# Attention values computed in pairs of steps, with one more buffer of exponentials and fewer of cross queries, in a kernel whose order comes from a list planner

## The chip, the cores and the metric

The kernel runs on one NeuronCore of a Trainium2 chip. The metric is the device time of one execution in microseconds, given as the median of several runs. A profile comes from one further execution of the same program, whose own time stands beside its span.

## The reference

Two blocks follow each other. The inputs are x (16 batches, 256 tokens, 256 features) and a context (16 batches, 77 tokens, 256 features), all in float32.

The first block is a transformer layer with 16 heads of 16 features:

```
h = x + attention(rmsnorm(x), rmsnorm(x))        # self, 256 keys
h = h + attention(rmsnorm(h), context)           # cross, 77 keys
h = h + (silu(n @ w_gate) * (n @ w_up)) @ w_down # n = rmsnorm(h), 1024 wide
attention: softmax(q k^T / 4) v per head, then @ wo
```

The second block takes h as queries and the context as keys and values. It normalizes both, attends with one head, squeezes through a layer of 4 features (gelu), attends among the 256 tokens of a batch with the result, and adds the parts to the normalized queries.

## The kernel before

**Units and batches.** Two batches make a unit of 512 tokens. The residual h of a unit stays in one of four buffers (`BUFS["h"]`, L82) from its load (L94) to its store (L1068). Everything else is per batch, except the cross keys and the final block, which work on a unit.

**Attention.** Queries and keys of a batch lie transposed, as two chunks of 128 features with 8 heads each. Each head pair takes 32 partitions. The partitions that the other head of the pair occupies are masked to zero, and one of them carries the row maximum as an extra product term.
- `self_operands` (L612) projects queries, keys and values (psq, psk, psv).
- `self_maxima` (L465) computes scores once for their maxima: four steps sc of 8 matmuls on row groups, each reduced on VectorE (L482). `cross_maxima` (L491) does the same with two steps csc.
- `maxima_rows` (L449) transposes the maxima (tm, ctm) and puts them into the queries.
- `exponentials` (L517) computes the scores again, with keys on partitions (st, cst), and ScalarE takes the exponential into a tile pT (L544). Self attention has four such steps per batch: two chunks of heads by two halves of the keys. Cross attention has two, one for each chunk, since 77 keys fit into one half.
- `outputs` (L549) multiplies values with exponentials (po, cpo), one step for each step of exponentials: 8 matmuls on column groups of the array, accumulated over the key halves in one bank, then a 32x32 transpose on VectorE (L576).
- `projection` (L578) divides by the sums, transposes and multiplies with wo (wo, cwo). `cross_queries` (L681) normalizes h, transposes (tp_ca) and projects cross queries (pscq), which ScalarE copies three times: into cqT as they are (L690), and masked into cqx (L692).

**MLP and final block.** `mlp` (L696) transposes (tp_mlp), multiplies with gate and up (pg, pu), passes tanh on ScalarE and two products on VectorE, and multiplies with down (wd). `second_context` (L860) and `second` (L896) make the final block, a long chain of small steps (tp_nF, xsc, tpxp, xav, tp_g2T, tp_mgT, lsc, lst, lav, tp_lav, out).

**PSUM.** There are eight banks: a tile of four for scores on row groups (`sc_banks`, one buffer, so each such step waits for the reading of the previous one), one for values (`po_bank`), and a ring of three for all else (`mm_bank`).

**The order.** Each stage is a generator that yields steps (`Step`, L223). A step states its duration on PE, its shape ("f" for the full array, "r" for row groups, "c" for column groups), its bank, its work on other engines, and the resources that it needs, takes and frees. `Order.run` (L310) picks at each point the PE step with the best key: steps that could start within a set waiting time (`wait`, L320) come first, then the rank. Ranks are the batch's number plus an offset by stage (`RANKS`, L1097), with further offsets for the first two and the last three batches. The buffers in `BUFS` limit how many tiles of a kind may be in flight. The four compute engines' queues then stand in exactly this order[...]. Loads and stores stand on SyncE's queue.

Three resources matter for the change. The ring of exponential tiles pT has two buffers, shared by self and cross attention. The resource "pair" (limit 1) keeps the exponentials of one group of steps from being mixed with another's: `acq` at the first key half, `rel` at the last. And the cross queries' tiles cqT and cqx have two buffers each.

Of the kernel before, what the change touches and what calls it, by code (L numbers as in the profile page):

```python
# [15 lines left out]
P = 128  # L16
D = 256
NC = D // P
# [4 lines left out]
UB = 2  # L23
RG = 32
# [5 lines left out]
def kernel(  # L30
# [10 lines left out]
    nc = tc.nc  # L41
    B, S, _ = x.shape
# [18 lines left out]
    def mm_bank(name):  # L61
        return ps_mm.tile([P, 512], F32, tag="mm", name=name)

    def po_bank(name):
        return ps_po.tile([P, 2, S], F32, tag="po", name=name)

    def sc_banks(name):
        return ps_sc.tile([P, 4, 512], F32, tag="sc", name=name)
# [8 lines left out]
    def tokens(ap, u):  # L77
# [2 lines left out]

    BUFS = {
        "h": 4, "cx": 1, "cx2": 2, "hn": 3, "hnT_sa": 1, "hnT_ca": 1, "hnT_mlp": 1, "ctxT": 1,  # L82
        "qx": 3, "kx": 3, "vone": 3, "cqT": 2, "cqx": 2, "ckm": 1, "ckx": 1, "cvone": 2, "pT": 2,
        "po": 1,
        "os": 2, "oq": 1, "oT": 1, "sg": 2, "gT": 1,
    }
# [129 lines left out]
    T_S, T_ST, T_CS, T_CST, T_PV = 816, 816, 478, 774, 740  # L216
# [6 lines left out]
    class Step:  # L223
        def __init__(self, pe=0, shape="f", bank="mm", ops=(), needs=(), acq=(), rel=(),
                     gives=(), order=None, free=False, lag=0, part=0):
            self.pe, self.shape, self.bank, self.ops, self.needs = pe, shape, bank, ops, needs
            self.acq, self.rel, self.gives = acq, rel, gives
            self.order, self.free, self.lag = order, free, lag

            self.part = part  # L230
# [6 lines left out]
    class Order:  # L237
# [72 lines left out]
        def run(self):  # L310
            while self.streams:
                best = None
                aux = []
                for st in self.streams:
                    t = self.start(st)
                    if t is None:
                        continue
                    if st.step.pe:

                        wait = 20 if "f" in (self.shape, st.step.shape) else 100  # L320
                        late = t > self.clock["P"] + wait
                        key = (late, t if late else 0, st.rank)
                        if best is None or key < best[0]:
                            best = (key, st, t)
                    else:
                        e = st.step.ops[0][0]
                        aux.append((max(t + T_NEXT, self.clock[e]), st.rank, st, t))
                if aux:
                    b, _, st, t = min(aux, key=lambda a: a[:2])
                    if best is None or b + sum(o[1] for o in st.step.ops) <= best[2] + best[1].step.pe + 800:  # L330
                        self.put(st, t)
                        continue
                assert best, [(st.rank, vars(st.step)) for st in self.streams]
                self.put(best[1], best[2])
# [95 lines left out]
    class Attention:  # L430
# [3 lines left out]
        def __init__(self, b, name, nk, w):  # L434
            self.b, self.name, self.nk, self.w = b, name, nk, w
            self.steps = [
                (c, kc, min(P, nk - kc * P)) for c in range(NC) for kc in range(-(-nk // P))
            ]
            self.q = self.k = self.qx = self.kx = self.v = None
            self.pT = {}  # L440

        def key(self, what, *more):
            return (self.name + what, self.b, *more)
# [44 lines left out]
    def last_of_pair(a):  # L488
        return a.b % UB == UB - 1
# [27 lines left out]
    def exponentials(a):  # L517

        b = a.b
        for k, (c, kc, nk) in enumerate(a.steps):  # L520
            last = k == len(a.steps) - 1
            rel = [(a.name + "qx", a.b)]
            if not a.name:
                rel.append(("kx", b))
            elif last_of_pair(a):
                rel.append(("ckx", b // UB))
            yield Step(
                T_CST if a.name else T_ST, "r", "sc", ops=[("A", 1870)], free=True,
                needs=[a.key("mT")] + [(a.name + "pT", b - 1, len(a.steps) - 1)] * (b > 0), acq=[("pT", a.name, a.b, k)] + [("pair",)] * (kc == 0),
                rel=[("pair",)] * (kc == (a.nk - 1) // P) + rel * last, gives=[a.key("pT", k)],  # L530
            )
            st = sc_banks(f"{a.name}st{a.b}_{k}")
            groups = [slice(RG * j, RG * (j + 1)) for j in range(4)]
            for e in range(2):
                for j, rg in enumerate(groups):
                    nc.tensor.matmul(  # L536
                        st[:nk, j, e * S : (e + 1) * S],
                        lhsT=a.kx[rg, c, e, kc * P : kc * P + nk], rhs=a.qx[rg, c, e],
                        start=True, stop=True,
                    )  # L540
            a.pT[k] = pool.tile(
                [P, 4, 2, S], F32, tag="pT", name=f"{a.name}pT{a.b}_{k}", bufs=BUFS["pT"]
            )
            nc.scalar.activation(  # L544
                a.pT[k][:nk].rearrange("p j e q -> p j (e q)"), st[:nk], AF.Exp,
                scale=HD ** -0.5,
            )

    def outputs(a):  # L549

        n = a.name
        for k, (c, kc, nk) in enumerate(a.steps):
            first, end = kc == 0, (kc + 1) * P >= a.nk
            yield Step(
                T_PV, "c", None, ops=[("V", 690)] if end else [], free=True,
                order=("pT", n, a.b, k), needs=[a.key("pT", k), a.key("v")],
                acq=[("po",)] * first + [("os", n, a.b)] * (end and c == 0),
                rel=[("pT", n, a.b, k)] + [("po",)] * end
                + [("cvone" if n else "vone", a.b)] * (k == len(a.steps) - 1),
                gives=[a.key("os", c)] * end,  # L560
            )
            if first:
                po = po_bank(f"{n}po{a.b}_{c}")
            pT = a.pT.pop(k)
            for e in range(2):
                for j in range(4):
                    nc.tensor.matmul(  # L567
                        po[RG * j : RG * (j + 1), e, :],
                        lhsT=a.v[:nk, kc, 8 * c + 2 * j + e, :], rhs=pT[:nk, j, e, :],
                        start=(first and e == 0), stop=end, skip_group_check=True,  # L570
                    )
            if end:
                if c == 0:
                    a.os = a.tile("os", [P, 2, NC, S], shared=True)

                nc.vector.transpose(a.os[:, :, c], po)  # L576

    def projection(a):  # L578

# [505 lines left out]
    def second_loads():  # L1085
# [4 lines left out]
    order = Order({**BUFS, "pair": 1})  # L1090
# [6 lines left out]
    RANKS = {  # L1097
        "loads": (-3, 0, 0),
        "second_constants": (1, 50, 0),
        "outputs": (1.5, 0, 0),  # L1100
        "exponentials": (-1.5, 0, 0),
        "projection": (1.25, 0, 0),
        "cross_outputs": (3, 0, 0),
        "cross_exponentials": (-50, 0, 0),
        "cross_projection": (-50, 0, 0),
        "self_maxima": (-1, 0, -50),
        "cross_maxima": (-49, 0, 0),
        "cross_queries": (1.75, 0, -1),
        "self_operands": (-1.5, 0, 1.5),
        "cross_keys": (2, 0, 0),  # L1110
        "mlp": (4.25, 0.25, -1),
        "second_context": (4, 0, -50),
        "second": (1, 0, 0),
    }

    def add(stage, b, tie, gen):
# [9 lines left out]
    for b in range(B):  # L1126
        a, ca = Attention(b, "", S, wo), crosses[b]
        add("outputs", b, 0, outputs(a))
        add("exponentials", b, 1, exponentials(a))
        add("projection", b, 2, projection(a))  # L1130
        add("cross_outputs", b, 0, outputs(ca))
        add("cross_exponentials", b, 1, exponentials(ca))
        add("cross_projection", b, 2, projection(ca))
        add("self_maxima", b, 1, self_maxima(a))
        add("cross_maxima", b, 1, cross_maxima(ca))
        add("cross_queries", b, 3, cross_queries(ca))
        add("self_operands", b, 5, self_operands(a))
        if b % UB == 0:
            add("cross_keys", b, 5, cross_keys(crosses[b : b + UB]))
        add("mlp", b, 4, mlp(b))  # L1140
# [43 lines left out]
```

## Time and profile before

| | |
|---|---|
| median of 3 runs | 1015.22 us (1014.69 to 1019.04) |
| profiled execution | 1016.78 us |
| its span, first to last instruction | 1015.0 us |
| mean granted TensorE clock | 0.985 |
| DVE reductions of sc (L482) | 64 of 2287 ns |
| exponentials of st (L544) | 64 of 1875 ns |
| exponentials of cst (L544) | 32 of 1872 ns |
| DMA | 17.58 MB, 16 engines mostly idle after the start |

The profile names an instruction by its line, engine, operation and tiles (output<-inputs), without buffer numbers. A float32 matmul is two records on PE, and a transpose is one; so "x8" of a projection is four matmuls of the program. In the timeline a row gives its start and its length in us, then what it is. The length of a PE row is modelled at its end, and rows overlap; the distance between the starts of two rows is what PE really takes. The slices show a span in 40 parts. In the chain of waits each piece is what the next one waited for.

### The profile page before, as it was taken

How to read it: one execution, taken by the hardware profiler on the slowest of the kernel's cores; microseconds unless marked ns; L12 is line 12 of the kernel's file. 1: busy time of each engine (PE TensorE's matmuls, PEld its weight loads, DVE VectorE, ACT ScalarE, POOL GpSimd, SP SyncE). 2: the span in 40 equal slices, each digit the busy share in tenths (PEclk: the TensorE clock that was granted, in tenths of full speed). 3: DMA queues.
4: the chain of work that ended last, by engine and by line, in shares of the span. 5: the costliest groups of instructions: out<-in, count | busy, mean ns of one | idle time of the engine just before them, and what ended most of it. 6: DMA issues, size and time to landing. Idle time of an engine off the chain costs nothing.

```text
span 1015.0 us, 18822 instructions
## 1 busy us (share of the span) xinstructions
PE 971.6 (96%) x8115; PEld 702.6 (69%) x8115; DVE 587.8 (58%) x1003; ACT 509.1 (50%) x876; POOL 80.7 (8%) x117
## 2 busy tenths in 40 slices
PE   6888899999999999999999999999999999999995
PEld 5655566767666777777777777767676777777872
DVE  3765674647775576645757356647466465345542
ACT  4545645452744626455373637553664627434432
POOL 2100000000100001000010001000010001000110
PEclk9999999999999999999999999999999999999995
DMA  9100000000000100010000100010000000000000
GB/s 297 34 1 7 1 1 2 2 8 1 1 8 8 43 1 8 2 43 1 7 2 13 42 1 1 7 43 1 8 8 2 22 1 2 1 22 1 2 21 22
DMA packets 17348, 17.58 MB, mean 17 GB/s; under 512 B 2832, under 2 KB 16752, under 8 KB 17264
## 3 DMA queue, kind: packets, MB, share of 16 engines
q1 hardware_dynamic: 16144, 15.32, 4.9%
q8 instruction: 64, 1.05, 0.4%
q10 hardware_dynamic: 1088, 1.05, 0.3%
q14 instruction: 20, 0.16, 0.1%
q0 software_dynamic: 32, 0.00, 0.0%
HBM read 12.13 MB, written 4.19 MB: 16 GB/s over the span
## 4 chain that ended last, share of the span: by engine, by line
PE 83%; DVE 8%; ACT 5%; DMA 3%; issue 1%; POOL 0%; ACTq 0%; POOLq 0%; SPq 0%
PE wd L746 11%; PE pu L717 10%; PE pg L717 10%; PE st L536 6%; PE sc L477 6%; PE po L567 5%; PE cst L536 3%; PE cwo L605 3%; PE psq L403 3%; PE cpo L567 3%; PE wo L605 3%; DVE nmax L482 2%; PE psv L637 2%; PE psk L403 2%; ACT pT L544 2%; PE pscq L403 2%
## 5 line engine op out<-in xcount | busy, mean ns | idle before, releaser
L482 DVE TENSOR_REDUCE nmax<-sc 128x8 f32<-128x2048 f32 x64 | 146.4, 2287 | 36.6 <-PE sc L477 36.5
L544 ACT ACTIVATE pT<-st 128x2048 f32<-128x2048 f32 x64 | 120.0, 1875 | 73.9 <-PE st L536 73.7
L717 PE MATMUL pg<-hnT_mlp,wg 128*128 128x256 f32 x512 | 129.3, 387 | 0.0
L717 PE MATMUL pu<-hnT_mlp,wu 128*128 128x256 f32 x512 | 128.5, 386 | 0.0
L746 PE MATMUL wd<-wd,gT 128*128 128x256 f32 x512 | 126.0, 387 | 0.0
L746 PEld LDWEIGHTS wd<-wd,gT 128*128 128x128 f32 x512 | 92.5, 190 | 23.5 <-issue 12.1
L717 PEld LDWEIGHTS pu<-hnT_mlp,wu 128*128 128x128 f32 x512 | 93.5, 190 | 20.3 <-issue 8.7
L717 PEld LDWEIGHTS pg<-hnT_mlp,wg 128*128 128x128 f32 x512 | 92.7, 190 | 20.0 <-issue 8.6
L727 ACT ACTIVATE sg<-pg 128x512 f32<-128x512 f32 x64 | 38.1, 596 | 98.0 <-PE pg L717 97.6
L544 ACT ACTIVATE cpT<-cst 77x2048 f32<-77x2048 f32 x32 | 59.9, 1872 | 54.5 <-PE cst L536 54.5
L728 DVE SCALAR_TENSOR_TENSOR sg<-sg,pg 128x512 f32<-128x512 f32 x64 | 43.9, 686 | 70.4 <-ACT sg L727 69.9
L567 PE MATMUL po<-pT,vone 128*32 128x256 f32 x1024 | 67.3, 391 | 0.0
L510 DVE TENSOR_REDUCE nmax<-csc 128x16 f32<-128x1232 f32 x32 | 46.1, 1441 | 17.1 <-PE csc L503 16.6
L729 DVE SCALAR_TENSOR_TENSOR gT<-sg,pu 128x512 f32<-128x512 f32 x64 | 43.6, 681 | 18.0 <-PE pu L717 17.2
L567 PEld LDWEIGHTS po<-pT,vone 128*32 128x32 f32 x1024 | 28.5, 111 | 28.8 <-issue 15.3
L751 DVE TENSOR_TENSOR h<-h,wd 128x256 f32<-128x256 f32 x32 | 13.3, 417 | 50.7 <-PE wd L746 50.6
L197 POOL TENSOR_TENSOR rstd_n<-ve_n,neg_half 128x4 f32<-128x4 f32 (+2 forms) x26 | 22.4, 862 | 242.2 <-DVE ve_n L195 235.5
L403 PE MATMUL psq<-hnT_sa,wq 128*128 128x256 f32 x128 | 34.8, 410 | 0.6 <-ACT hnT_sa L363 0.6
L567 PE MATMUL cpo<-cpT,cvone 77*32 77x256 f32 x512 | 34.3, 385 | 0.3 <-DVE cos__7617 L576 0.3
L403 PE MATMUL psk<-hnT_sa,wk 128*128 128x256 f32 x128 | 32.6, 390 | 0.0
L403 PE MATMUL pscq<-hnT_ca,cwq 128*128 128x256 f32 x128 | 32.4, 390 | 0.0
L197 POOL TENSOR_TENSOR rstd_ca<-ve_ca,neg_half 128x2 f32<-128x2 f32 x16 | 11.1, 694 | 263.2 <-DVE ve_ca L195 263.2
(601 smaller groups left out, 1567.2 us busy)
## 6 DMA issues: line engine op xcount, KB each, us to landing
h<-in_x_dram SPq DMA_DIRECT2D x7, 512.0 KB
out_dram<-h SPq DMA_DIRECT2D x7, 512.0 KB
cx<-in_ctx_dram SPq DMA_DIRECT2D x16, 154.0 KB
wg<-in_L_xattn_w_gate_dram SPq DMA_DIRECT2D x1, 1024.0 KB
wu<-in_L_xattn_w_up_dram SPq DMA_DIRECT2D x1, 1024.0 KB
wd<-in_L_xattn_w_down_dram SPq DMA_DIRECT2D x1, 1024.0 KB
h<-in_x_dram SPq DMA_DIRECT2D x4, 128.0 KB
out_dram<-h SPq DMA_DIRECT2D x2, 256.0 KB
```

The lines of the kernel that those rows point to most:

```text
L403: nc.tensor.matmul(ps[:, m * n : (m + 1) * n], lhsT=w[:, c, m * P : (m + 1) * P], rhs=srcT[:, c, :], start=(c == 0), stop=(c == NC - 1),)
L477: nc.tensor.matmul(sc[:, j, (1 - e) * S : (2 - e) * S], lhsT=a.qx[rg, c, e, qt * P : (qt + 1) * P], rhs=a.kx[rg, c, e], start=True, stop=True,
L482: nc.vector.tensor_reduce(maxima_of(nm, qt)[:, :, c::NC], sc.rearrange("p j (y k) -> p j y k", y=2), AX.X, ALU.max, negate=True,)
L510: nc.vector.tensor_reduce(maxima_of(nm, qt), sc[:, :, : 2 * NC * SK].rearrange("p j (n k) -> p j n k", k=SK), AX.X, ALU.max, negate=True,)
L536: nc.tensor.matmul(st[:nk, j, e * S : (e + 1) * S], lhsT=a.kx[rg, c, e, kc * P : kc * P + nk], rhs=a.qx[rg, c, e], start=True, stop=True,)
L544: nc.scalar.activation(a.pT[k][:nk].rearrange("p j e q -> p j (e q)"), st[:nk], AF.Exp, scale=HD ** -0.5,)
L567: nc.tensor.matmul(po[RG * j : RG * (j + 1), e, :], lhsT=a.v[:nk, kc, 8 * c + 2 * j + e, :], rhs=pT[:nk, j, e, :], start=(first and e == 0 ...
L605: nc.tensor.matmul(ps[:, i * D : (i + 1) * D], lhsT=oT[:, c, i * P : (i + 1) * P], rhs=a.w[:, c, :], start=(c == 0), stop=(c == NC - 1),)
L717: nc.tensor.matmul(ps[:, i * S : (i + 1) * S], lhsT=w[:, c, (f + i) * P : (f + i + 1) * P], rhs=hnT[:, c, :], start=(c == 0), stop=(c == N ...
L728: nc.vector.scalar_tensor_tensor(sg, sg, 1.0, ps, ALU.add, ALU.mult)
L729: nc.vector.scalar_tensor_tensor(gT[:, f : f + 2, :].rearrange("p f q -> p (f q)"), sg, 0.5, banks[1], ALU.mult, ALU.mult,)
L746: nc.tensor.matmul(ps[:, :D], lhsT=gT[:, f, i * P : (i + 1) * P], rhs=wd[:, f, :], start=(f == 0), stop=(f == NF - 1),)
```

## The change

It changes five things.

1. `outputs` makes a step out of `per_visit` single steps: one for the first two batches, two for all others. For self attention a step then holds both key halves of a chunk, which accumulate in one bank. For cross attention it holds both chunks of heads: the first goes to the values' bank as before, the second to a bank of the mm ring, and both are transposed by VectorE behind the step.
2. The ring of exponential tiles has three buffers. The cross query tiles cqT and cqx have one each.
3. The resource "pair" in `exponentials` spans as many steps as `pair` says: two where it was two (self) and one or two for cross attention.
4. The waiting rule is exchanged: 100 ns where a full-array shape is involved, otherwise 20.
5. The ranks have new offsets.

```diff
-        "qx": 3, "kx": 3, "vone": 3, "cqT": 2, "cqx": 2, "ckm": 1, "ckx": 1, "cvone": 2, "pT": 2,
+        "qx": 3, "kx": 3, "vone": 3, "cqT": 1, "cqx": 1, "ckm": 1, "ckx": 1, "cvone": 2, "pT": 3,
...
-                        wait = 20 if "f" in (self.shape, st.step.shape) else 100
+                        wait = 100 if "f" in (self.shape, st.step.shape) else 20
...
+            self.per_visit = 1 if b < UB else 2
...
+        pair = max(a.per_visit, len(a.steps) // NC)
...
-                needs=[a.key("mT")] + [(a.name + "pT", b - 1, len(a.steps) - 1)] * (b > 0), acq=[("pT", a.name, a.b, k)] + [("pair",)] * (kc == 0),
-                rel=[("pair",)] * (kc == (a.nk - 1) // P) + rel * last, gives=[a.key("pT", k)],
+                needs=[a.key("mT")] + [(a.name + "pT", b - 1, len(a.steps) - 1)] * (b > 0), acq=[("pT", a.name, a.b, k)] + [("pair",)] * (k % pair == 0),
+                rel=[("pair",)] * (k % pair == pair - 1) + rel * last, gives=[a.key("pT", k)],
...
         n = a.name
-        for k, (c, kc, nk) in enumerate(a.steps):
-            first, end = kc == 0, (kc + 1) * P >= a.nk
+        per = a.per_visit
+        for k0 in range(0, len(a.steps), per):
+            steps = list(enumerate(a.steps))[k0 : k0 + per]
+            ends = [c for _, (c, kc, _) in steps if (kc + 1) * P >= a.nk]
+            first = steps[0][1][1] == 0
             yield Step(
-                T_PV, "c", None, ops=[("V", 690)] if end else [], free=True,
...
+                T_PV * per, "c", "mm" if len(ends) > 1 else None, ops=[("V", 690)] * len(ends),
...
+            for k, (c, kc, nk) in steps:
+                if kc == 0:
+                    if k == k0:
+                        po = po_bank(f"{n}po{a.b}_{c}")
+                    else:
+                        po = mm_bank(f"{n}po{a.b}_{c}").rearrange("p (e q) -> p e q", e=2)
...
-        "outputs": (1.5, 0, 0),
-        "exponentials": (-1.5, 0, 0),
-        "projection": (1.25, 0, 0),
-        "cross_outputs": (3, 0, 0),
+        "outputs": (1.5, -1, 50),
+        "exponentials": (-3.5, 0, 1),
+        "projection": (1.25, -50, 0),
+        "cross_outputs": (3, 0, 0.25),
         "cross_exponentials": (-50, 0, 0),
-        "cross_projection": (-50, 0, 0),
-        "self_maxima": (-1, 0, -50),
+        "cross_projection": (-50, 0, 50),
+        "self_maxima": (0, 0, -100),
         "cross_maxima": (-49, 0, 0),
-        "cross_queries": (1.75, 0, -1),
-        "self_operands": (-1.5, 0, 1.5),
-        "cross_keys": (2, 0, 0),
-        "mlp": (4.25, 0.25, -1),
-        "second_context": (4, 0, -50),
-        "second": (1, 0, 0),
+        "cross_queries": (2, 0, 0.5),
+        "self_operands": (-0.5, 0, 1.5),
+        "cross_keys": (2.5, 0, 0),
+        "mlp": (4.25, -0.25, -0.5),
+        "second_context": (5, 0, -50),
+        "second": (2, 0, 0),
```

More of the change, by code (lines that the diff above doesn't have):

```diff
@@ L551, in outputs @@
         n = a.name
-        for k, (c, kc, nk) in enumerate(a.steps):
-            first, end = kc == 0, (kc + 1) * P >= a.nk
-            yield Step(
-                T_PV, "c", None, ops=[("V", 690)] if end else [], free=True,
[L556 to L560, printed above, removed]
-            )
[L562 to L576, printed above, removed]
@@ new lines, in outputs @@
+        per = a.per_visit
[3 more added lines that the diff above has]
+            first = steps[0][1][1] == 0
+            yield Step(
+                T_PV * per, "c", "mm" if len(ends) > 1 else None, ops=[("V", 690)] * len(ends),
+                free=True, order=("pT", n, a.b, k0),
+                needs=[a.key("pT", k) for k, _ in steps] + [a.key("v")],
+                acq=[("po",)] * first + [("os", n, a.b)] * (0 in ends),
+                rel=[("pT", n, a.b, k) for k, _ in steps] + [("po",)] * (len(ends) > 0)
+                + [("cvone" if n else "vone", a.b)] * (NC - 1 in ends),
+                gives=[a.key("os", c) for c in ends],
+            )
+            for k, (c, kc, nk) in steps:
[4 more added lines that the diff above has]
+                        po = mm_bank(f"{n}po{a.b}_{c}").rearrange("p (e q) -> p e q", e=2)
+                pT, end = a.pT.pop(k), (kc + 1) * P >= a.nk
+                for e in range(2):
+                    for j in range(4):
+                        nc.tensor.matmul(
+                            po[RG * j : RG * (j + 1), e, :],
+                            lhsT=a.v[:nk, kc, 8 * c + 2 * j + e, :], rhs=pT[:nk, j, e, :],
+                            start=(kc == 0 and e == 0), stop=end,
+                            skip_group_check=True,
+                        )
+                if end:
+                    if c == 0:
+                        a.os = a.tile("os", [P, 2, NC, S], shared=True)
+                    nc.vector.transpose(a.os[:, :, c], po)
```

## The prediction

> **What bounds the kernel now.** I read the page first: engine shares, slices, chain.
>
> ```profile
> span 1015.0 us, 18822 instructions
> ...
> PE 971.6 (96%) x8115; PEld 702.6 (69%) x8115; DVE 587.8 (58%) x1003; ACT 509.1 (50%) x876; POOL 80.7 (8%) x117
> ...
> PE   6888899999999999999999999999999999999995
> ...
> PEclk9999999999999999999999999999999999999995
> ...
> PE 83%; DVE 8%; ACT 5%; DMA 3%; issue 1%; POOL 0%; ACTq 0%; POOLq 0%; SPq 0%
> ```
>
> PE is busy almost everywhere and carries 83% of the chain. So the time is PE's own row-to-row spacing plus the stalls at the two ends. A busy share does not say what a row costs, because matmul records overlap. I therefore took the timeline of PE and used the distance from one row's start to the next row's start.
>
> ```profile
> 641.58 1.89 PE L717 MATMUL pu<-hnT_mlp,wu 128*128 128x256 f32 x8
> 643.40 1.10 PE L536 MATMUL cst<-ccqx__5203,cckx__5073 32*77 32x256 f32 x16
> 644.44 1.06 PE L950 MATMUL xav<-nXf,xpT 77*128 77x5 f32 x8
> ...
> 649.75 1.89 PE L717 MATMUL pu<-hnT_mlp,wu 128*128 128x256 f32 x8
> 651.48 1.89 PE L717 MATMUL pg<-hnT_mlp,wg 128*128 128x256 f32 x8
> 653.20 1.03 PE L717 MATMUL pu<-hnT_mlp,wu 128*128 128x256 f32 x4
> ...
> 655.35 1.07 PE L567 MATMUL cpo<-cpT,cvone 77*32 77x256 f32 x16
> 656.35 0.71 PE L1016 MATMUL lsc<-mgT,g2T 32*128 32x256 f32 x8
> 657.00 1.99 PE L746 MATMUL wd<-wd,gT 128*128 128x256 f32 x8
> 658.83 0.38 PE L1004 MATMUL tp_mgT<-ident,mga 128*128 128x128 f32 x2
> ```
>
> Eight records of a full-array matmul take 1.73 us when another full-array row stands on both sides (649.75 to 651.48). They take 1.82 us when a row-group step follows (641.58 to 643.40), and 1.83 us when such a step came before (657.00 to 658.83). So entering a tiled shape costs about 93 ns. Leaving one costs about 104 ns ahead of a plain matmul, and 56 ns ahead of a transpose (437 to 493 ns for four). A single step of values (16 records, column groups) takes 1.00 us (655.35 to 656.35). Two back to back show this:
>
> ```profile
> 341.85 1.94 PE L567 MATMUL po<-pT,vone 128*32 128x256 f32 x32
> 343.71 1.10 PE L536 MATMUL cst<-ccqx__2786,cckx__2144 32*77 32x256 f32 x16
> ```
>
> A pair takes 1.86 us, so a step followed by another one takes 0.863 us. The last one of a visit pays a further 0.138 us.
>
> I took the least spacing of each kind of row and added it over the whole PE order. That gives 948.0 us of work. The first row starts at 6.2 us, and 4.9 us follow the last one. The remaining 55.9 us are stalls: 25.4 up to 125 us (weights loading, few batches in flight, two stretches of 3.4 us at half clock), 12.0 from 125 to 960 us, and 18.5 in the tail, where the last unit's dependent chain runs alone. One of the stalls in the middle has its cause in the chain by time:
>
> ```profile
> 328.64 1.23 DVE h L1067
> ...
> 329.89 4.22 DMA out_dram<-h
> ...
> 334.17 3.38 DMA h<-in_x_dram
> ...
> 337.64 0.52 ACT sq_sa L345 x2
> ...
> 338.72 0.17 DVE ve_sa L195
> 338.89 1.35 DVE nmax L510
> ```
>
> The tokens of unit 4 can only be loaded once unit 0 is stored (four h buffers, L92). DVE's ve_sa waits for them, the cross maximum stands behind it in DVE's order, and PE idles 0.79 us at 339.4. The same follows the next two stores: 0.4 us at 455.8 and 1.1 us at 581 to 583.
>
> [...]
>
> **The change, part by part.** The changed kernel issues the same matmuls, evacuations and DMAs; the built orders have equal counts for every tile. Only the order, the buffers and one destination bank differ.
>
> *Steps of values in pairs.* From batch 2 on, self attention does both key halves in one step, and cross attention does both head chunks. Counted in the two PE orders (lav's column steps included), neighbouring column steps rise from 17 to 43. That is 26 x 0.138 = 3.6 us saved. Visits that start from a full-array row fall from 241 to 230: 11 x 0.093 = 1.0 us. Exits are 177 to plain matmuls and 63 to transposes before, and 182 and 47 after: 21.9 - 21.6 = 0.3 us. One more neighbouring pair of row-group steps saves 0.26 us (816 against 1076 ns). The sum is 5.2 us of PE work, all on the path, since PE is the bound. For the cross pairs (14) the second half goes to another bank, which no pair of before shows. [...]14 x 0.138 = 1.9 us would be lost again. Nothing in the trace suggests that, and a gain beyond 0.863 us per step isn't to be had, as it is the spacing inside a pair. I take 0 and keep 1.9 for the range.
>
> *Third buffer of exponentials.* It adds no instruction. It lets the third exponential run before a pair of values has freed two buffers. In the order of before, from 125 us on, the shortest PE work between scores and their values is 3.0 us, and the observed need is about 3.1 (1.88 of exponential, the scores' own 1.08, the hand-over). After it is 5.3 us. So the pairs shouldn't wait for exponentials. Without the buffer that cover would be gone: a pair would hold both buffers, and each third score step would wait for the pair. PE's waits for pT before self scores are 1.4 us in all from 125 to 960 us, in the wait view, and bound the gain. I book 0.
>
> *Cross values in the mm ring.* 14 second halves take one of three banks until a DVE transpose of 0.72 us. In the new order the third-next user starts at least 2.6 us after the start of such a half, which needs 1.0 of matmuls, 0.72 of transpose and some 0.2 of hand-over, so 0.7 is to spare: 0. If DVE comes 1.2 us late at half of them, 7 x 0.5 = 3.5 us would be left over.
>
> *Single cqT and cqx.* A batch's cross query projection has to wait for the previous batch's last cross scores. In the order of before, batch 3 overtakes batch 2 by 5 us. In the new order the shortest distance is 4.3 us, the others 8 to 40. ACT's three copies (about 0.6 and twice 0.69 us) come after that. So the wait is added in name and is satisfied on arrival: 0. Queued behind it on ACT would be exponentials and the MLP's tanh, for which PE waits.
>
> *Ranks and the waiting rule.* These move steps. The final stage comes earlier against the next load: from the last output row of a unit to the transpose of the batch that its buffer lets in, PE has 12.7, 13.9 and 12.7 us of work before, and 41.8, 40.7 and 40.7 after. Store, load and norm need 13.5 (observed). SP's queue holds the same transfers, one context load ahead of a store here and there, with more than 25 us to spare. POOL's row scaling of 2.36 us (L922) moves with the final stage, and the norms' powers (0.69 us) queue behind it as before: 0, inside the queueing below. So the three load stalls go: 0.8 + 0.4 + 1.1 = 2.3 us. What is late next are distances that the new order makes short. From 125 us to the tail I compared each with its observed need: first projection behind an MLP transpose 1.2, 1.3 us (need 1.9), behind a cross transpose 1.6, 1.6 (1.9), transposes behind lsc 1.6 (2.3), MLP transpose behind the cross projection 5.4 (5.7), score bank behind sc 3.5, 3.5 (3.7). Shortfalls: 1.3 + 0.6 + 0.7 + 0.3 + 0.4 = 3.3, against about 1.1 of the same kinds before. That is +2.2 us. The head is the same row for row for the first 36 us of PE work. After that the shortfalls of score banks come to 17.9 us against 17.8 before over the first 125 us: 0. The tail's chain is the same rows: 0. What is left of the middle's 12 us is queueing at DVE, ACT and POOL that distances do not show. It may fall or rise by some 4 us.
>
> **Sum.** -5.2 - 2.3 + 2.2 = -5.3 us. Span 1015.0 becomes 1009.7. The profiled execution took 1016.78 us, 1.8 more than its span, and stands 1.6 above the median of 1015.22 (runs 1014.69 to 1019.04). From the median: 1009.9 us.
>
> **Rivals.** *More is won.* The wider distances (5.3 us before values) also absorb the queueing in the middle, up to half of its 12 us, and the head gives one of its half-clock windows back (1.7 us): 1009.9 - 6 = 1004. For it: exponentials are no longer tight before values. Against it: the maxima's transposes now stand only 2.0 us ahead of the first scores, where they had 4.8. *The stalls take it back.* Turns are saved, but the time goes into waits for VectorE, since steps that were spread out now come in bunches: two transposes of 0.72 us behind each cross pair, with maxima of 2.29 us in the same queue. 14 x 0.3 us from that alone, or the bank's 1.9 with it: about 1015. In this case the visits are fewer in the trace, and the time is not. *Slower.* With one cqx, ACT reaches a cross copy before its buffer is free, and exponentials and tanh queue behind it. The place is the hand-over from one batch to the next, 15 times. To end above 1020.3 it must eat the 5.3 and add 5.1, so it decides from 10.4 / 15 = 0.7 us at each. At 0.9 us the time is 1023. Against it: 14 of the 15 distances are above 8 us.
>
> **Chances.** Forecast, 1006 to 1013.5: 0.48. More won, below 1006: 0.27. Taken back, 1013.5 to 1020: 0.18. Slower: 0.07. About 0.5% (5.1 us) is what a measurement tells from no change here, so the border is 1010.1. It cuts the forecast's case a little above its middle: faster 0.48 x 0.55 + 0.27 = 0.53, slower 0.07, within 0.5% 0.40. The range from 1002 to 1016 leaves out the slower case, a third of the case that takes back, and a quarter of the first rival, some 0.2 together. It includes the bank's 1.9, the ring's 3.5 and the queueing's 4 us.
>
> **What would show it.** In the profile after: "po" rows mostly of 32 records, 1.86 us to the next row; "cpo" likewise, whatever the bank[...]. No store-then-load on the chain from 300 to 600 us. Work by spacing near 942.8 us, and stalls between 125 us and the tail near 12. Waits of PE on "hn_mlp", "hnT_ca" and "hnT_mlp" a little longer. It would be wrong if the head's stalls changed by over 4 us, if ACT waited for cst ahead of L690, or if a half-clock window appeared in the middle.

## The result and the profile after

The changed kernel takes 1011.26 us (median of 8 runs, 1009.32 to 1014.26), the kernel before 1016.76 in the same 8 rounds. The ratio is 0.9946, with a 95% interval of 0.9928 to 0.9965: 5.5 us less, where 5.3 were forecast. The profiled execution took 1009.76 us, with a span of 1008.0; it is the second fastest of the eight.

The page of the changed kernel, the same lines as before: span, engines, slices of PE and of its clock, the chain by engine.

```profile
span 1008.0 us, 18781 instructions
...
PE 967.5 (96%) x8115; PEld 708.6 (70%) x8115; DVE 584.4 (58%) x1003; ACT 509.4 (51%) x876; POOL 80.6 (8%) x117
...
PE   6888899999999999999999999999999999999994
...
PEclk9998999999999999999999999999999999999995
...
PE 86%; DVE 6%; ACT 4%; DMA 3%; issue 1%; POOL 0%; POOLq 0%; ACTq 0%; SPq 0%; DVEq 0%
```

The counts of instructions on all five rows are the same. PE is still the bound. One slice in the head has a lower clock than before.

The distances between the starts of PE's rows, summed as in the prediction, split both spans. Work is the least distance of each kind of row, added up over all rows; a stall is what a row took beyond that:

| us | before | after |
|---|---|---|
| work by spacing | 948.0 | 942.9 |
| stalls up to 125 us | 25.4 | 26.3 |
| stalls from 125 to 960 us | 12.0 | 9.5 |
| stalls after 960 us | 18.5 | 18.4 |
| ahead of the first row and after the last | 11.1 | 10.9 |

So 5.1 of the span's 7.0 us are work that PE no longer does, and 2.5 are stalls in the middle. The head gave 0.9 us back. Its half-clock stretches are 6.8 and 3.4 us long here, and were twice 3.4 us before. The table is of one execution each; the medians are 5.5 us apart.

### The profile page after: what moved, and what is told of

It reads as the page before. It is cut to its first block, busy times and chain, and to the rows that moved or that the text cites. A ratio compares the mean times of both kernels' runs of the same rounds, so it can differ in the third digit from the quotient of the medians.

```text
span 1008.0 us, 18781 instructions
## 1 busy us (share of the span) xinstructions
PE 967.5 (96%) x8115; PEld 708.6 (70%) x8115; DVE 584.4 (58%) x1003; ACT 509.4 (51%) x876; POOL 80.6 (8%) x117
## 4 chain that ended last, share of the span: by engine, by line
PE 86%; DVE 6%; ACT 4%; DMA 3%; issue 1%; POOL 0%; POOLq 0%; ACTq 0%; SPq 0%; DVEq 0%
PE wd L760 12%; PE pu L731 11%; PE pg L731 11%; PE st L538 7%; PE sc L477 6%; PE po L580 5%; PE cst L538 3%; PE cwo L619 3%; PE psq L402 3%; PE pscq L402 2%; PE wo L619 2%; PE cpo L580 2%; PE csc L503 2%; PE psk L402 2%; DVE nmax L482 2%; PE psv L651 2%
## 5 line engine op out<-in xcount | busy, mean ns | idle before, releaser
L731 PE MATMUL pg<-hnT_mlp,wg 128*128 128x256 f32 x512 | 131.4, 391 | 0.7 <-ACT hnT_mlp L362 0.7
L580 PE MATMUL po<-pT,vone 128*32 128x256 f32 x1024 | 63.5, 386 | 0.6 <-ACT pT L546 0.6
L580 PEld LDWEIGHTS po<-pT,vone 128*32 128x32 f32 x1024 | 29.9, 110 | 26.2 <-issue 9.9
L651 PE MATMUL psv<-wv,hnT_sa 128*128 128x256 f32 x128 | 31.4, 385 | 0.0
L580 PE MATMUL cpo<-cpT,cvone 77*32 77x256 f32 x512 | 31.4, 383 | 0.0
```

Of the source, the lines that this page charges most:

```text
L580: nc.tensor.matmul(po[RG * j : RG * (j + 1), e, :], lhsT=a.v[:nk, kc, 8 * c + 2 * j + e, :], rhs=pT[:nk, j, e, :], start=(kc == 0 and e == ...
L651: nc.tensor.matmul(ps[:, t * D : (t + 1) * D], lhsT=hnT[:, c, t * P : (t + 1) * P], rhs=wv[:, c, :], start=(c == 0), stop=(c == NC - 1),)
L731: nc.tensor.matmul(ps[:, i * S : (i + 1) * S], lhsT=w[:, c, (f + i) * P : (f + i + 1) * P], rhs=hnT[:, c, :], start=(c == 0), stop=(c == N ...
```

## The experiments

All ratios are to the kernel before in the same rounds: 4 to 6 runs of a variant, 22 of two of them. Changes in us are the ratio's share of some 1016.5 us. A change from one variant to another carries both intervals, 2 to 2.6 us either way.

### What a break between two halves costs

A full-array matmul of one column goes between the two halves of each cross pair, ahead of the real ones that overwrite its output.

```diff
                         po = mm_bank(f"{n}po{a.b}_{c}").rearrange("p (e q) -> p e q", e=2)
+                        nc.tensor.matmul(
+                            po[:, 0, :1], lhsT=ident, rhs=ident[:, :1], start=True, stop=True
+                        )
```

> The changed kernel in its own order, with one full-array matmul of a single column between the two halves of each of the 14 cross pairs (its output is overwritten; the results are the same). Theory[...]: each costs 93 + 104 + 138 ns and some 0.05 to 0.15 us of its own, 14 x 0.43 = 6.0 us over the changed kernel, so about the time of before. Rival (a step costs what its instructions cost, and the shape is no matter): 14 x 0.1 = 1.4 us over the changed kernel, 4 us under before.

Measured: 0.9987 (0.9979 to 0.9995), 4.2 us more than the changed kernel. The timeline of PE in this kernel, at one of the 14 places:

```profile
315.08 1.07 PE L583 MATMUL cpo<-cpT,cvone 77*32 77x256 f32 x16
316.08 0.38 PE L577 MATMUL cpo<-ident 128*128 128x1 f32 x2
316.39 1.07 PE L583 MATMUL cpo<-cpT,cvone 77*32 77x256 f32 x16
317.39 0.71 PE L1033 MATMUL out<-last,g2T 32*128 32x256 f32 x8
```

The first half now takes 1.00 us up to the next row, and the one-column matmul 0.31 us. Without it, a cross pair in the changed kernel looks like this:

```profile
436.15 1.93 PE L580 MATMUL cpo<-cpT,cvone 77*32 77x256 f32 x32
438.01 1.15 PE L477 MATMUL sc<-kx__3660,qx__3639 32*128 32x256 f32 x16
```

That is 1.86 us for 32 records in two banks. So a break costs 1.00 + 0.31 - 0.86 = 0.45 us, 6.3 us for 14. Of these, 4.2 arrive in the time. The rest fell into stalls: without the breaks themselves, those between 125 and 960 us are 7.7 us here, where the changed kernel has 9.5. The rival's 1.4 us is out. Two further answers: a change of bank costs nothing here (all 14 cross pairs take 1.86 us; with 0.138 us for the change, the 1.9 us that the forecast kept for its range, each would take 2.00), and the forecast's 0.138 us per neighbouring step holds for cross pairs too. This is the one test of the turns that leaves the order as it is.

### Each part alone, and each part undone

Pairs, third buffer and single cross queries with the old ranks and the old waiting rule:

```diff
-                        wait = 100 if "f" in (self.shape, st.step.shape) else 20
+                        wait = 20 if "f" in (self.shape, st.step.shape) else 100
...
-        "outputs": (1.5, -1, 50),
-        "exponentials": (-3.5, 0, 1),
...
+        "outputs": (1.5, 0, 0),
+        "exponentials": (-1.5, 0, 0),
...
```

> The changed kernel with the old ranks and the old waiting rule: pairs of value steps, three exponential buffers and single cross queries alone; the planner makes a new order from them. Counted in that order, PE's work by spacing is 943.3 us against 948.0 before. Theory (the turns decide): 4.8 us less than before, stalls about as before, so -3 to -7 us. Rival (the gain came from the ranks, which took the load stalls and the queueing away): within 2 us of before.

Measured: 1.0056 (1.0044 to 1.0068), 5.7 us slower. Both expectations missed. The work is 943.3 us as counted, but the stalls are 66.7 us (before 55.9): 31.9 in the head, with three stretches at half clock, one of them 13.7 us long, 14.7 in the middle, and 20.2 in the tail.

The reverse, ranks and waiting rule on the kernel before:

```diff
-                        wait = 20 if "f" in (self.shape, st.step.shape) else 100
+                        wait = 100 if "f" in (self.shape, st.step.shape) else 20
...
-        "outputs": (1.5, 0, 0),
...
+        "outputs": (1.5, -1, 50),
...
```

> The kernel before with the new ranks and the new waiting rule alone: single steps, two exponential buffers, two buffers for cross queries. Its order has 254 entries into tiled shapes and 5 neighbouring column steps, and 952.2 us of work by spacing, 4.2 more than before. Theory (the turns decide): +2 to +6 us against before, the load stalls' 2.3 us given back. Rival (the ranks made the gain): -3 to -5 us.

Measured: 1.0119 (1.0103 to 1.0134), 12.1 us slower, beyond the theory's range. Work as counted 952.2 us, stalls 65.0. The rival is out.

The changed kernel with single steps:

```diff
-            self.per_visit = 1 if b < UB else 2
+            self.per_visit = 1
```

> The changed kernel with single steps of values for all batches (ranks, waiting rule, three exponential buffers and single cross queries kept); the planner orders anew. Work by spacing in that order is 950.9 us, 8.0 more than in the changed kernel, with 251 entries into tiled shapes instead of 230. Theory (turns, on top of an order whose stalls decide as much): +8 us over the changed kernel for the turns and 0 to +7 for stalls, so +3 to +10 us against before. Rival (the third buffer and the ranks made the gain, pairs are incidental): within 3 us of the changed kernel.

Measured: 1.0165 (1.0150 to 1.0181), 16.8 us slower than before. Work as counted 950.9 us, stalls 70.8. The rival is out; the count has the theory's 8 us of turns, and its stalls were set far too low.

The changed kernel with two exponential buffers:

```diff
-        ... "ckx": 1, "cvone": 2, "pT": 3,
+        ... "ckx": 1, "cvone": 2, "pT": 2,
```

> The changed kernel with two exponential buffers as before; pairs, ranks and waiting rule kept. Work by spacing is 944.1 us, 1.1 more than in the changed kernel. Theory (the third buffer is the cover that keeps pairs from waiting; without it a pair holds both buffers and the third score step stands behind it): 5 to 10 us over the changed kernel, nearly all as stalls between 125 and 960 us. Rival (exponentials run early enough with two): 1 to 2 us over the changed kernel.

Measured: 1.0059 (1.0042 to 1.0076), 6.0 us slower than before and 11.5 over the changed kernel, above the theory's 5 to 10 by less than the noise. Work 944.1 us. The stalls in the middle are 22.6 us, where the changed kernel has 9.5: the place is the theory's. Some 1.6 us of them are a half-clock stretch at 854 us, behind the longest wait. Waits of PE between 125 and 960 us, in this kernel (who waits for whom, us in total, times, longest):

```profile
PE cst L538 <- ACT cpT L546: 2.4, 2, 2.3
PE csc L503 <- DVE nmax L510: 1.8, 2, 1.1
PE sc L477 <- DVE nmax L482: 1.5, 2, 1.2
PE csc L503 <- ACT pT L546: 1.3, 2, 1.1
```

The same view of the changed kernel:

```profile
PE pscq L402 <- ACT hnT_ca L362: 0.8, 2, 0.4
PE cwo L619 <- DVE coT__5714 L610: 0.8, 1, 0.8
PE pg L731 <- ACT hnT_mlp L362: 0.7, 1, 0.7
```

With two buffers, the longest waits are for score banks that ScalarE and VectorE have not yet read. With three, no wait for a score bank is among the longest. The theory's own picture, a score step behind a pair that holds both buffers, is not what these waits show: the planner keeps to the buffers by laying another order, and in it some score steps come before their bank has been read.

The changed kernel with the old waiting rule:

```diff
-                        wait = 100 if "f" in (self.shape, st.step.shape) else 20
+                        wait = 20 if "f" in (self.shape, st.step.shape) else 100
```

> The changed kernel with the old waiting rule alone (20 ns where a full-array shape is involved, 100 otherwise). Work by spacing is 942.8 us, the same as in the changed kernel, with 231 entries and 44 neighbouring column steps. Theory A (the rule only guards the turns): within 1.5 us of the changed kernel. Theory B (the order that it happens to give has closer distances, 13 us of shortfalls in the middle where the changed kernel has 7, and 3.5 more in the head): 4 to 9 us over the changed kernel.

Measured: 1.0083 (1.0067 to 1.0098), 14 us over the changed kernel, with the same work (942.8 us). Theory A is out, and B's size was exceeded: stalls 29.9 us in the head and 20.4 in the middle, with two stretches at half clock in the head and three more up to 202 us.

These five have one thing in common. PE's work in them is counted from each built order, and the stalls are what is left of the trace's span (from the kernel before to the changed one, the counts give 5.2 us less work and the trace's timeline 5.1). The time did not follow the work, since each edit makes the planner lay another order, with 9 to 15 us more of stalls than before. The gain is a property of the whole order that was built, not of any of its parts, and none of the five isolates its part.

Some of the added stalls are the clock's. Ahead of the tail, the half-clock stretches of a trace add up to 6.8 us before, to 10.2 in the changed kernel, to 20.5 with the pairs alone and with the old waiting rule, and to 13.7 in the other three. A row takes about twice as long in them (st 2.02 us against 1.08, shown below). By this estimate the clock adds up to 6.8 us of stalls against before in the two, and 3.4 in the three. For the pairs alone that is more than the 5.7 us by which they are slower. No run holds the clock up in these five orders, so their price at full clock is not shown.

### The loads

The kernel before, then the changed kernel, with a fifth buffer for h that the planner doesn't count. The order on PE, DVE, ACT and POOL stays the same; SyncE issues each later load of x one unit earlier. In both, a small tile of the start-up gives up its second buffer, and in the second one two tiles of the final stage share memory.

```diff
-            hs[u] = hpool.tile([P, NT, D], F32, tag="h", name=f"h{u}", bufs=BUFS["h"])
+            hs[u] = hpool.tile([P, NT, D], F32, tag="h", name=f"h{u}", bufs=5)
```

> The kernel before with a fifth buffer for h that the planner doesn't know of, so that the order on PE, DVE, ACT and POOL stays word for word the same; each later load of x goes out one unit earlier (one small buffer of the start-up goes from two to one to make room). Theory (the store and the load behind it cost the stalls at 339, 456 and 582 us): -2.3 us, those stalls gone. Rival (they only happened to lie there, and DVE's queue is late anyway): within 0.7 us of before.

Measured: 0.9981 (0.9974 to 0.9988), 1.9 us less than before. The stalls in the middle fall from 12.0 to 9.6 us. The timeline of PE at the first of the three stalls, in the kernel before:

```profile
339.45 0.27 PE L454 MATMUL ctm<-ident,nmax 128*128 128x128 f32 x1
340.29 0.33 PE L454 MATMUL ctm<-ident,nmax 128*128 128x128 f32 x1 [0.57 <-DVE nmax L510]
```

The same place with the fifth buffer:

```profile
338.19 1.03 PE L717 MATMUL pu<-hnT_mlp,wu 128*128 128x256 f32 x4
339.06 0.38 PE L454 MATMUL ctm<-ident,nmax 128*128 128x128 f32 x2
339.28 1.03 PE L717 MATMUL pu<-hnT_mlp,wu 128*128 128x256 f32 x4
```

The two transposes follow each other without the 0.57 us of idle time that stood between them. The stalls at 456 and 582 us are gone too, and the others of the middle stay. The theory holds.

But the chain of the changed kernel still has these loads, which the prediction said it would not. From its chain by time:

```profile
430.96 4.84 DMA out_dram<-h
...
435.82 3.64 DMA h<-in_x_dram
...
439.54 0.52 ACT sq_sa L344 x2
...
440.08 0.51 ACT sq_sa L344 x2
440.59 0.73 ACT hnT_ca L362 x2
...
441.37 1.13 PE pscq L402 x4
```

The sum of squares of the next unit (sq_sa) stands in ScalarE's queue ahead of hnT_ca, and waits for the load; ScalarE is idle for 2.70 us ahead of it. PE is stopped by hnT_ca, not by anything of the new unit. The stalls at 439.9 (0.65 us), 558.7 (0.58) and 675.9 (0.93, by VectorE's ve_sa) are the three loads again: 2.2 us, against 2.3 before.

> The changed kernel with a fifth buffer for h that the planner doesn't know of, in its own order on all engines, each later load of x one unit earlier (room is made by letting two small tiles of other stages share memory). Theory (the load stalls did not go away with the change: the norm of the next batch still stands in ScalarE's and VectorE's queue right behind the load, and the stalls at 440, 559 and 676 us are these): 1.5 to 3 us under the changed kernel, those three stalls gone. Rival (the final stage now comes 40 us ahead of the load's use, so loads no longer cost): within 0.7 us of the changed kernel.

Measured: 0.9914 (0.9900 to 0.9928), 3.3 us under the changed kernel. PE's timeline in the changed kernel:

```profile
439.85 1.07 PE L619 MATMUL wo<-wo,oT__3642 128*128 128x256 f32 x4
441.37 1.13 PE L402 MATMUL pscq<-hnT_ca,cwq 128*128 128x256 f32 x4 [0.44 <-ACT hnT_ca L362]
```

And in this kernel:

```profile
440.82 0.65 PE L205 MATMUL tp_ca<-ident,hn_ca 128*128 128x128 f32 x4
441.31 0.43 PE L885 MATMUL tpx<-ident,cx 77*128 77x77 f32 x4
441.58 1.07 PE L619 MATMUL wo<-wo,oT__3642 128*128 128x256 f32 x4
442.49 1.04 PE L402 MATMUL pscq<-hnT_ca,cwq 128*128 128x256 f32 x4
```

From wo to pscq it takes 0.91 us here, and 1.52 in the changed kernel. All three stalls are gone; those of the middle fall from 9.5 to 7.2 us. The rival is out.

### The clock in the head and in the tail

Matmuls that nobody reads (fillers) go into stalls, in the order as it is. In the changed kernel's head:

```diff
+    def filler(n):
+
+        ps = mm_bank("filler")
+        for _ in range(n):
+            nc.tensor.matmul(ps[:, :D], lhsT=ident, rhs=wq[:, 0, :], start=True, stop=True)
+
...
+            if a.b == 1 and qt == 1:
+                filler(3)
             sc = sc_banks(f"csc{a.b}_{qt}")
...
+            if not a.name and b == 1 and k == 3:
+                filler(4)
             st = sc_banks(f"{a.name}st{a.b}_{k}")
```

> The changed kernel in its own order with matmuls that nobody reads in two stalls of the head: four (1.7 us) in the one of 2.33 us at 81 us, three (1.3 us) in the one of 1.9 us at 112 us. Theory (the two half-clock stretches of 6.8 and 3.4 us that follow come from PE's low activity, and they cost 2 to 4 us): both stretches gone or shorter, 2 to 4 us under the changed kernel. Rival (PE waits for ScalarE and VectorE there anyway, the clock is no matter): between 0 and 1 us over it.

Measured: 0.9900 (0.9882 to 0.9917), 4.7 us under the changed kernel by the ratios, somewhat more than the 2 to 4 expected. The changed kernel's timeline in the head:

```profile
81.23 1.15 PE L538 MATMUL st<-qx__298,kx__319 32*128 32x256 f32 x16
84.37 2.09 PE L538 MATMUL st<-qx__298,kx__319 32*128 32x256 f32 x16 [2.00 <-ACT pT L546]
86.39 1.94 PE L580 MATMUL po<-pT,vone 128*32 128x256 f32 x16
```

The same with the extra matmuls:

```profile
80.95 1.15 PE L548 MATMUL st<-qx__298,kx__319 32*128 32x256 f32 x16
82.03 1.99 PE L495 MATMUL filler<-wq,ident 128*128 128x256 f32 x8
84.09 1.15 PE L548 MATMUL st<-qx__298,kx__319 32*128 32x256 f32 x16
85.17 1.07 PE L590 MATMUL po<-pT,vone 128*32 128x256 f32 x16
```

The second st starts as long after the first as it did (3.14 us), so the filler cost nothing. Then st takes 1.08 instead of 2.02 us up to the next row. Both half-clock stretches of the head are gone in this profile: the mean clock from 78 to 90 us is 1.00 where the changed kernel has 0.72, and from 112 to 125 us 1.00 for 0.87.

The same in the kernel before, at its own two stalls:

```diff
+            if a.b == 0 and qt == 0:
+                filler(3)
             sc = sc_banks(f"csc{a.b}_{qt}")
...
+            if not a.name and b == 1 and k == 1:
+                filler(4)
             st = sc_banks(f"{a.name}st{a.b}_{k}")
```

> The kernel before in its own order, with matmuls that nobody reads in two stalls of its head: four in the one of 2.33 us at 69 us, three in the one of 1.7 us at 84 us, ahead of its two half-clock stretches of 3.4 us. Theory (the clock of the head is a cost of its own, beside the turns): both stretches gone, 3 to 5.5 us under before, and the changed kernel with such matmuls stays 5 to 7 us under this one. Rival (the change moved the head's stalls in a way that only its own order can gain from): within 1 us of before.

Measured: 0.9965 (0.9951 to 0.9979), 3.6 us under before. The changed kernel with fillers is 6.6 us under this one, as expected. That is what the change is worth with both heads at full clock in the profiled executions. The scatter shrinks too: the five executions with fillers lie between 1012.77 and 1013.31 us, and the nine without, in the same rounds, between 1015.59 and 1019.04 (mean clocks 0.986 to 0.987, and 0.982 to 0.988).

With fillers in the waits of the last unit's chain as well:

```diff
+        def tail(count, since=NU):
+            if n >= since:
+                po = po_bank(f"tail{n}")
+                for _ in range(count):
+                    nc.tensor.matmul(
+                        po[:, 0, :], lhsT=ident, rhs=wq[:, 0, :], start=True, stop=True
+                    )
...
+        tail(6)
         g2T = by_token([g], "g2T")
```

> The changed kernel with the matmuls that nobody reads in the head's two stalls, and with more of them in the waits of the last unit's chain (one to six of 0.43 us each, shorter than the stall that they stand in). Theory (the 26 us at half clock in the tail double PE's parts of that chain): the tail keeps the full clock, 1 to 3 us less than with the head's matmuls alone, so 12 to 14 us under before. Rival (that chain is made of hand-overs of VectorE and ScalarE, and the extra matmuls only stand in the way): 0 to 2 us more than with the head's alone.

Measured: 0.9861 (0.9843 to 0.9879), 4.0 us under the head's fillers alone, where the theory had 1 to 3. The end of the kernel with the head's fillers alone (its length, then PE, PEld, DVE, ACT, POOL busy, PE's clock, the DMA share and GB/s):

```profile
950.00:1004.00 54.00, 39.11 (x186) 28.48 (x184) 18.39 (x59) 17.41 (x34) 5.32 (x6) 0.75 0.06 20
```

The same with fillers in the tail too:

```profile
950.00:1000.00 50.00, 43.75 (x228) 32.41 (x226) 17.95 (x59) 17.34 (x34) 5.32 (x6) 0.97 0.07 22
```

PE's mean clock there goes from 0.75 to 0.97, and DVE, ACT and POOL have about the same to do.

Fillers and the fifth buffer together:

> The changed kernel with the fifth buffer for h and with the matmuls that nobody reads in the stalls of head and tail: all causes that the runs pointed to, together. If they are independent: 14.7 us of the head's and tail's matmuls and 2 us of the loads under before, so about 1000 us.

Measured: 0.9853 (0.9834 to 0.9873), 15 us under before (16.7 if all parts were independent) and not told apart from the version without the fifth buffer. The runs form two groups: 1000.6 to 1000.8 us at a mean clock of 0.999, and 1004.7 to 1004.8 at 0.996. The profiled one is of the second group, and has two half-clock stretches of 3.4 us in the head again, at 70 and 84 us. So two fillers don't prevent them in every execution. The fillers stand ahead of the stretches that the changed kernel's profile has, at 83 and 117 us; with the fifth buffer alone, in the same order on PE, the stretches were at 71, 88 and 119. This version is, with the one before it, the fastest found.

## Why the prediction came out right, point by point

**Turns, -5.2 us: right.** PE's work fell from 948.0 to 942.9 us, and cross pairs take 1.86 us in two banks as in one. The break between halves shows the price directly, for 14 of the 26 new neighbours.

**Third buffer, booked at 0: no wait for exponentials is among the longest, as forecast.** Without it the time is 11.5 us longer, nearly all in the middle. But that is another order, like the one with the old waiting rule (14 us) and the one with single steps (22 us), so it is no price of the buffer by itself.

**Loads, -2.3 us: wrong.** The step that failed is that "the three load stalls go" because PE has 40 us of work between a unit's last output and the transpose of the batch that its buffer lets in. What matters is not that distance. ScalarE comes to the norm's first operation 5.7 to 5.9 us after the store's start, and the store and the load take 6.9 to 8.5 us in the chain. It then stands idle for 2.7, 2.6 and 1.3 us, with steps of other batches queued behind the norm, and these are late. The stalls are 2.2 us, where none were forecast, and the fifth buffer takes them away. The place to read was that of sq_sa in ScalarE's order, not only that of tp_sa in PE's.

**Shortfalls, +2.2 us: half right.** Found are 0.79 us ahead of the MLP's first projection at 914.5, 0.31 at 913.7 ahead of csc, and 0.65 behind lsc at 944.2: 1.75, against the 1.1 of before that the prediction set off, so some +0.65. The two cross projections that stand only 1.6 us behind their transposes did stall, but the cause was the load: with the fifth buffer they show no stall, so their need of 1.9 us was set too high.

**Queueing, booked at 0 within 4 us: fell by about 3.** The stalls at 275 us (1.19; an MLP norm waiting for VectorE and GpSimd ahead of an exponential) and 303 us (0.92; a table load of 1.28 us ahead of an exponential) in the kernel before have no counterpart. In the middle, then, the loads came out 2.2 us dearer than forecast, and shortfalls and queueing together 4.6 us cheaper; these errors cancelled in part. The span fell by 7.0 us and the median by 5.5. That the sum of 5.3 met the median within 0.2 us is partly luck, the more so as the interval of that ratio is 1.9 us either way.

**Single cross queries: 0, right.** The shortest time from a batch's last cst to the next batch's copy into cqT is 6.8 us in the trace. No wait for it was seen.

**Head, booked at 0: nearly.** It lost 0.9 us in the profile, with 10.2 us at half clock instead of 6.8. PE was partly busy ahead of each of these stretches. In the changed kernel its rows cover 2.12 of the 3.41 us up to the stretch at 82.9 us, and 1.84 of the 3.41 us up to the one at 117.0. In the kernel before they cover 1.41 up to the stretch at 72.9 us, and 1.78 up to the one at 86.6. Half clock followed each time.

In each of these two traces the half-clock stretches start whole multiples of 3.413 us apart: at 72.91, 86.57 and 991.10 us before (4 and 265 times), at 82.91, 117.05 and 984.03 us after (10 and 254 times). The lengths of rows are modelled, so the cover is only a sign. The changed kernel's rows cover 2.02 of the 3.41 us from 110.2 us on, less than the 2.12 ahead of the stretch at 82.9, and the next 3.41 us were at full clock. So the cover does not tell by itself which stall is followed by half clock, and what does is not shown.

**The rivals.** "Slower" by a blocked copy has no trace in this order. "The stalls take it back" did not happen to the change as built, but it is what happened in the three other orders that keep the pairs (old ranks and rule, two buffers, old rule). Of "more is won", one half came true: queueing fell by 3 us. The head gave no half-clock stretch back.

What stays open is why exactly each variant's order stalls more; only the places and the engines waited for were read. Runs of the changed kernel differ (1009.3 to 1014.3 us), and the two slowest have the lowest mean clocks, 0.978 and 0.980 where the other six have 0.981 to 0.983. That fits more half-clock stretches, but only one of these executions was profiled.

## What to carry to other kernels

Where PE is the bound, take its cost from the distances between starts of rows, by kind of row and by the shape of the neighbours; summed over a built order, it foretold the change in work to 0.1 us. An order from a planner is one object: change a rule, a buffer or a rank alone, and the stalls of the new order can outweigh what the edit saves. For a load, look at the first instruction that needs it in the queue where it stands, and at what is queued behind it, rather than at the first use on the bounding engine.

## What the runs showed of the hardware

- The half-clock stretches in the head lasted 3.41 or 6.83 us in the profiles before and after, and their starts lie whole multiples of 3.413 us apart in each. PE's rows cover 1.41 to 2.12 of the 3.41 us ahead of each stretch. Four matmuls without use in such a stall (1.7 us in one of 2.33) went with a mean clock of 1.00 from 78 to 90 us, where it was 0.72, and the next row started as long after the one before (3.14 us). The stretches lie elsewhere from trace to trace (83 and 117 us in the changed kernel; 71, 88 and 119 with the fifth buffer), and fillers set for one profile did not keep the clock in every execution (0.999 in three runs with fillers and buffer, 0.996 in two).
- Two column-group steps in different banks take 1.86 us for 32 records, as two in one bank do; with one single-column matmul of another shape between them it is 0.45 us more.
- A chain of small dependent steps at the end of the kernel ended 4.0 us sooner when fillers in its waits raised PE's mean clock from 0.75 to 0.97.
- Norms that waited for their loads held up what was queued behind them on ScalarE and VectorE (ScalarE idle for 2.7, 2.6 and 1.3 us): 2.2 us of stalls of PE at three loads, gone with one more buffer.
